# Searching step two's row tiles among eight logits per 128-column chunk, and the rest in three listed tiles

## The chip, the cores and the metric

The kernel runs on one core of a Trainium2 chip. The metric is the device time of one execution in microseconds; the number given for a kernel is the median over its runs. A profile is one further execution, recorded instruction by instruction. The engines are PE (TensorE), DVE (VectorE), ACT (ScalarE), POOL (GpSimd) and SP (SyncE, which here issues most DMAs).

## What is computed

Two graph layers over N = 4096 nodes with 256 features. Layer 0 is a dense graph attention and is not touched by the change. Layer 1 does two diffusion steps along two paths:

```python
def _top_p_attention(X, W1, W2, W3):
    q = X @ W1.T @ W2.T
    k = X @ W3.T
    logits = q @ k.T / TAU
    probs = jax.nn.softmax(logits, axis=-1)
    idx = jnp.argsort(-probs, axis=-1)
    sp = jnp.take_along_axis(probs, idx, axis=-1)
    cs = jnp.cumsum(sp, axis=-1)
    keep_sorted = cs - sp < TOP_P            # 0.9
    mask = ...                               # scattered back
    A = probs * mask
    return A / jnp.maximum(A.sum(-1, keepdims=True), 1e-12)

R = S + eye; R = R / R.sum(-1)               # S is the adjacency
for n in range(2):
    A = _top_p_attention(Xa, W1, W2, W3)
    Xf = R @ Xf                              # "mixing"
    Xa = A @ Xa                              # "row tiles"
    Z = Z + Xf @ U1[n].T + Xa @ U2[n].T
h = X + Z; layer norm; add X; layer norm
```

For each row of the attention matrix the smallest set of probabilities that sums to 0.9 (the nucleus) has to be found. On the reference's inputs a row of step one keeps 4.8 entries on average, one of step two 30 (median 12, the largest 846).

## The kernel before

`graph_attention` is layer 0. `nucleus_layer` is layer 1, and its work is laid out by a plan: `at(time, part, ...)` enters each part of each tile with a due time in units of a step-one tile, `carry_out()` sorts the entries, and the instructions of PE, ACT, DVE and POOL are issued in that order (`tc.manual_schedule`). So the due times of the dictionaries `T1`, `T2` and `TE` are an order and no clock: each engine runs its own instructions in the order written and waits on semaphores. SP has its own queue of DMAs, in the order in which the parts issue them.

Step one handles 28 row tiles as `EasyTile` (the eight largest logits of a row, gathered), then nine "dense" tiles as `RowTile(0, ...)`: the last four and five with rows that eight entries did not cover. The rows of these five are found by `HardRows`: a flag for each row, ranks by matmuls with triangular and full matrices (`count`), a list of row numbers (`place`, `enter`, `keep`, `read_list`), and an indirect DMA that gathers the listed rows (`load_hard`). A dense tile of step one computes 4096 logits a row (L1105) and keeps the eight largest of each chunk of 128 columns (`tops`, L1115). It searches the threshold among these 256 candidates alone: two estimates (`under`, L1201), a mask (`final`), three rounds of eight maxima (`sort`, L1311 and L1313), `edge`, and then one pass over all 4096 columns that keeps what reaches the edge (`select`, L1362).

Step two runs 32 tiles `RowTile(1, i)`, 128 rows each, over all 4096 columns (`place_second`). For each tile: logits, eight blocks of 512 (PE L1105, ACT L1110); the maximum over 4096 (`top`, L1122); exponentials and their sums (ACT, L1129 and L1140); three estimates of the threshold, on a quarter of the columns, on ACT's half (`estimate_half`, L1213 and L1216, four passes over 2048) and on half (`estimate`, L1201); `final`, a mask of 4096 columns into the single buffer `w`; `tops` over `w`; six rounds of `sort`; `edge`; `inside` (ranks among the 256 candidates, for ties); `cut`, which takes the kept candidates out of `w` chunk by chunk (32 replaces of eight values, L1371) and subtracts `w` from `p` on POOL (L1375, four of 1024 columns); then 32 transposes (L1383) with copies on ACT (L1396) and 32 products against `xa` (L1405, two passes each) into `ap`. `product_out` scales the rows and stores them into `xa2_d`.

Beside the tiles runs the mixing: `Group(n, g)` covers 512 columns of the adjacency; each of its 32 steps loads a block of `adj32_d` (256 KB) and one of `adj_d` in 8 bits (64 KB) into one of three buffers each (L1678), and PE does two pairs of matmuls (L1713): the rows in 16 bits against the 8-bit block, the rest against the 32-bit block. Step two holds the last six groups of the first mixing and all eight of the second. When a group of the second is done, `Out` finishes its four tiles: `product_y` and `sum_y` (the mixed part, into `h_d`), then `product` for both attention parts, two layer norms (mostly small POOL operations) and the store. At the end a count of rows whose search did not hold is read (`flag`); only if it isn't zero does a general path run after it (`missed`).

Of the kernel before, what the change touches and what calls it, by code (L numbers as in the profile page):

```python
# [8 lines left out]
F32 = mybir.dt.float32  # L9
# [13 lines left out]
P = 128  # L23
# [62 lines left out]
def tile_graph_layers(  # L86
# [60 lines left out]
    xa1_d = dram.tile([N + P, D], F32, name="xa1_d")  # L147
    src_d = dram.tile([2, H, N], F32, name="src_d")
# [8 lines left out]
    def lengthen(part):  # L157
# [13 lines left out]
        xf, room, x1_d, xa2_d, xa1_d, narrow, shares, flag, out,  # L171
# [3 lines left out]
    missed = nc.values_load(flag[0:1, 0:1], min_val=0, max_val=2 * STEPS * N)  # L175
# [642 lines left out]
ROOM = HARD * P  # L818
# [3 lines left out]
def nucleus_layer(  # L822
    ctx, tc, adjT, adj_d, adj32_d, y_d, h_d, high_d, low_d, w1, w2, w3, kT, U1T, U2T, ln_g, ln_b, ident, eps,
    xf, room, x1_d, xa2_d, xa1_d, narrow, shares, flag, out,
# [79 lines left out]
    junk_v = one.tile([P, N // 2], U8, name="junk_v")  # L904

# [3 lines left out]
    SEARCHED = FIRST + NT  # L909
# [8 lines left out]
    def spare(length):  # L918
# [21 lines left out]
    nc.gpsimd.memset(every, 1.0)  # L940
    nc.gpsimd.affine_select(
        before, every, pattern=[[1, P]], compare_op=ALU.is_gt, fill=0.0, base=0, channel_multiplier=-1
    )
    sums_before = [one.tile([P, FEW + 1], F32, name=f"sums_before{k}") for k in range(3)]
    for t in sums_before:
        nc.gpsimd.memset(t[:, 0:1], 0.0)
    is_hard = one.tile([P, EASY], F32, name="is_hard")
    nc.gpsimd.memset(is_hard, 0.0)
    BATCH = 7

    def counted(name, pattern, base, step=0):
# [6 lines left out]
    ids = counted("ids", [[P, EASY]], 1, 1)  # L958
    places = spare(P)
    nc.gpsimd.iota(  # L960
        places, pattern=[[1, P]], base=-ROOM, channel_multiplier=0, allow_small_or_imprecise_dtypes=True
    )
    steps = counted("steps", [[P, HARD - 1]], P - ROOM)
    blocks = counted("blocks", [[1, HARD]], 0)
    beyond = counted("beyond", [[0, 1]], N + 1, 1)
    listed = one.tile([P, HARD], F32, name="listed")
    hard_ids = one.tile([P, HARD], I32, name="hard_ids")
    sources = one.tile([P, HARD], I32, name="sources")
    unused = one.tile([P, HARD], F32, name="unused")
    fits = one.tile([P, 1], F32, name="fits")  # L970
# [68 lines left out]
    class RowTile:  # L1039


        def __init__(self, n, i, hard=None):
            self.n, self.i, self.hard = n, i, hard
            self.id = f"{n}_{i}" if hard is None else f"{n}_h{hard}"
            self.at = FIRST + i if n else i - EASY if hard is None else OWN + hard
            self.est = EST[n]
# [5 lines left out]
        @property  # L1052
        def own(self):
            return self.cur[:, self.i, :] if self.hard is None else hx[:, self.hard, :]
# [64 lines left out]
        def top(self):  # L1119
            self.ntop = self.tiny("ntop")  # L1120
            src = self.p if self.n else self.cand
# [30 lines left out]
        def scalars(self):  # L1152
# [10 lines left out]
            self.aim = self.tiny("aim", aims[self.n].shape[1])  # L1163
            nc.vector.tensor_scalar(self.aim, aims[self.n], self.rz, None, ALU.mult)
            self.set_goal(0)

        def scalars2(self):
            q, z = self.q_row, all_z[:, self.at, :]
            self.gain = self.tiny("gain", len(self.est) + 1)
            nc.vector.tensor_scalar(self.gain, gains[self.n], q, None, ALU.mult)  # L1170
# [4 lines left out]
            if self.n == 0:  # L1175
# [19 lines left out]
        def under(self, dst, sub=1):  # L1195

            src = self.cand if self.n == 0 else self.p
# [24 lines left out]
        def estimate(self, k):  # L1222
            self.b = self.under(junk_v, (4, None, 2)[k] if self.n else 1)
# [7 lines left out]
        def join(self, k):  # L1231
            b, share = self.b, 0 if self.n and k == 0 else None
            if self.n and k:
# [13 lines left out]
        def move(self, k):  # L1247
# [4 lines left out]
            if last and self.n:  # L1252
# [35 lines left out]
        def lift(self):  # L1288

            f = self.tiny("f")  # L1290
            nc.vector.tensor_scalar(f, self.t, self.rz, ALONE[self.n], ALU.mult, ALU.is_ge)
# [3 lines left out]

        def final(self):
            b = self.under(w)
            self.r = self.tiny("r")
            nc.vector.tensor_scalar(self.r, b, self.left, None, ALU.add)


        def sort(self, k):
            rounds = ROUNDS[self.n]
            if k == 0:
                self.src = w[:, : NC * TOP] if self.n == 0 else self.cand
                self.rest_of = two.tile(
                    [P, NC * TOP], F32, tag="left", name=f"left{self.id}", bufs=1
# [1255 lines left out]
```

## Time and profile before

| | us |
|---|---|
| median of 8 runs | 3193.47 |
| lowest, highest | 3180.82, 3209.27 |
| the profiled execution | 3194.15 |
| its span, first to last instruction | 3192.4 |

Busy time of the engines by stage of the profiled execution, in us:

| stage | window | PE | DVE | ACT | POOL | DMA share |
|---|---|---|---|---|---|---|
| graph attention | 0 to 950 | 839 | 812 | 748 | 102 | 0.67 |
| step one, easy tiles | 950 to 1325 | 333 | 328 | 282 | 246 | 0.43 |
| step one, dense tiles | 1325 to 1500 | 162 | 148 | 150 | 27 | 0.10 |
| keys of step two | 1500 to 1641 | 121 | 33 | 38 | 14 | 0.45 |
| step two | 1641 to 3192 | 1350 | 1335 | 1117 | 596 | 0.40 |

Times count from the first instruction. A row of the groups of instructions reads: line, engine, operation, what it writes and reads, shape and count, then busy us and the mean ns of one, then the engine's idle time before it and what ended that. A row of the timeline reads: start, length, engine, line, operation, names, shape and count, and in brackets idle time before it. Matmuls are pipelined, so that their rows overlap.

### The profile page before, as it was taken

Reading aid. Unit: us, or ns where it says so; the run is one execution under the profiler, and the core shown is the slowest. Engines: PE = TensorE matmul, PEld = TensorE weight load, DVE = VectorE, ACT = ScalarE, POOL = GpSimd, SP = SyncE. Lnnn points to the kernel's source line nnn. Section 1 sums busy time; section 2 is a strip of 40 time slices with the busy share of each in tenths; the row PEclk is TensorE's granted clock in tenths of the full one; section 3 lists DMA queues with packets and bytes.
Section 4 is the critical chain, followed back from the end, with each engine's and each line's share of the span. In section 5 each row is a group of like instructions: output and inputs, shape, how many; then the busy total and the mean of one; then the engine's idle time right before and its main releaser. Section 6 shows DMA issues by size and latency. Waiting matters only on the chain.

```text
span 3192.4 us, 48261 instructions
## 1 busy us (share of the span) xinstructions
PE 2804.6 (88%) x15876; PEld 1690.0 (53%) x15876; DVE 2656.4 (83%) x6811; ACT 2335.0 (73%) x3521; POOL 985.1 (31%) x1102
## 2 busy tenths in 40 slices
PE   7999887898888998699967998997998989989975
PEld 4432222222225665487634666665666766766754
DVE  4769998999987999787128999999988888888983
ACT  4668987898876787797247777778766777777762
POOL 1101141000005777412002233324235354454553
PEclk8989999999989999799988999999999999999987
DMA  9988867653214444201544444463444444444410
GB/s 240 241 203 253 223 225 244 224 195 110 86 57 125 132 138 131 76 23 51 178 140 133 131 131 128 136 193 95 127 130 133 134 135 136 138 138 137 134 54 23
DMA packets 298853, 451.68 MB, mean 141 GB/s; under 512 B 34528, under 2 KB 174816, under 8 KB 295520
## 3 DMA queue, kind: packets, MB, share of 16 engines
q1 hardware_dynamic: 278528, 401.04, 38.0%
q0 software_dynamic: 20064, 47.47, 8.8%
q8 instruction: 127, 2.08, 0.3%
q14 instruction: 134, 1.10, 0.1%
HBM read 447.06 MB, written 127.14 MB: 180 GB/s over the span
## 4 chain that ended last, share of the span: by engine, by line
PE 29%; DVE 20%; ACT 8%; POOL 4%; issue 3%; DMA 2%; SPq 0%; DVEq 0%; POOLq 0%; ACTq 0%
PE ap L1405 9%; PE rp L1713 7%; DVE w L1371 4%; DVE c L1115 2%; PE tpa L1383 2%; PE ap_h L1405 2%; DVE ntop L1122 2%; DVE junk_v L1201 2%; DVE w L1201 2%; POOL p L1375 2%; ACT junk_s L1213 1%; PE zpo L1796 1%; PE lp L1105 1%; PE ape L1513 1%; DVE tie L1466 1%
## 5 line engine op out<-in xcount | busy, mean ns | idle before, releaser
L1405 PE MATMUL ap<-xa,at 128*128 128x257 f32 x2048 | 502.4, 389 | 38.9 <-ACT at L1396 38.6
L676 DVE COPY_PREDICATED other<-mask,e 128x2048 f32<-128x2048 uint8 x176 | 453.8, 2590 | 52.9 <-ACT other L661 45.1
L1713 PE MATMUL rp<-adj,low 128*128 128x512 f32 x896 | 474.0, 591 | 9.9 <-DMA adj<-adj_d 9.7
L1405 PEld LDWEIGHTS ap<-xa,at 128*128 128x128 f32 x2048 | 383.2, 193 | 102.6 <-ACT at L1396 49.0
L654 ACT ACTIVATE e<-src,minus_flat,factors 128x2048 f32<-128x2048 f32 x176 | 367.8, 2090 | 64.8 <-DVE other L676 34.7
L706 PE MATMUL acc<-other,v 128*32 128x512 f32 x2816 | 344.4, 607 | 77.2 <-DVE other L676 58.3
L1713 PE MATMUL rp<-short,p 128*128 128x512 fp8e4 x896 | 352.6, 394 | 22.2 <-POOL short L1695 18.3
L661 ACT ACTIVATE other<-away,minus_flat 128x2048 f32<-128x2048 f32 x176 | 350.6, 1992 | 7.1 <-PE acc L706 4.5
L1375 POOL TENSOR_TENSOR p<-p,w 128x1024 f32<-128x1024 f32 x128 | 299.8, 2366 | 128.3 <-DVE w L1371 119.8
L1371 DVE MATCH_REPLACE8 w<-c,w 128x128 f32<-128x128 f32 x1024 | 267.7, 275 | 0.0
L1396 ACT COPY at<-tpa 128x512 f32<-128x512 f32 x280 | 161.4, 579 | 129.9 <-PE tpa L1383 128.8
L706 PEld LDWEIGHTS acc<-other,v 128*32 128x32 f32 x2816 | 80.6, 110 | 295.6 <-DVE other L676 137.4
L1105 PE MATMUL lp<-kT,q 128*128 128x512 f32 x576 | 185.9, 442 | 44.2 <-ACT p L1110 29.6
L1713 PEld LDWEIGHTS rp<-adj,low 128*128 128x128 f32 x896 | 180.1, 201 | 61.0 <-issue 20.1
L679 DVE COPY_PREDICATED e<-mask,away 128x2048 f32<-128x2048 uint8 x80 | 208.5, 2606 | 2.6 <-DMA mask<-mask_d 2.5
L1115 DVE MAX8 c<-w 128x8 f32<-128x128 f32 x1024 | 200.8, 275 | 0.0
L1383 PE MATMUL tpa<-ident,p 128*128 128x128 f32 x1152 | 179.0, 280 | 24.3 <-POOL p L1375 12.3
L706 PE MATMUL acc<-other,ones 128*32 128x512 f32 x1408 | 186.1, 601 | 0.0
L1129 ACT ACTIVATE junk_s<-p,htop 128x2048 uint8<-128x2048 f32 x72 | 144.3, 2004 | 48.3 <-DVE htop L1124 48.3
L1383 PEld LDWEIGHTS tpa<-ident,p 128*128 128x128 f32 x1152 | 145.5, 145 | 62.3 <-POOL p L1375 15.2
L1503 POOL DMA_INDIRECT p<-x_d,tie x152 | 158.0, 1039 | 66.2 <-issue 21.2
L1713 PEld LDWEIGHTS <-p 128*128 128x128 f16 x896 | 87.4, 98 | 166.9 <-issue 159.3
(429 smaller groups left out, 5982.2 us busy)
## 6 DMA issues: line engine op xcount, KB each, us to landing
adj<-adj_d SPq DMA_DIRECT2D x448, 256.0 KB
mask<-adj_d SPq DMA_DIRECT2D x164, 256.0 KB
short<-adj_d SPq DMA_DIRECT2D x448, 64.0 KB
adj<-in_adjT SPq DMA_DIRECT2D x64, 256.0 KB
mask<-mask_d SPq DMA_DIRECT2D x60, 256.0 KB
mask<-in_adjT POOLq DMA_DIRECT2D x32, 256.0 KB, 9.4
src<-src_d SPq DMA_DIRECT2D x8, 1024.0 KB
away<-src_d SPq DMA_DIRECT2D x8, 1024.0 KB
```

The costliest lines, as they stand in the source:

```text
L654: nc.scalar.activation(self.e, self.head.src, AF.Relu, scale=self.factor(0), bias=self.factor(2))
L661: nc.scalar.activation(self.other, self.head.away, AF.Identity, bias=self.factor(2))
L676: nc.vector.copy_predicated(self.other, self.mask, self.e)
L679: nc.vector.copy_predicated(self.e, self.mask, self.other)
L706: nc.tensor.matmul(head.acc[k][at : at + 32, :], weights, self.e[:, b * 512 : (b + 1) * 512], tile_position=(0, at), **ends,)
L1105: nc.tensor.matmul(lp, self.q[:, k], kT[:, b * 512 : (b + 1) * 512], start=k == 0, stop=k == 1)
L1115: nc.vector.max(self.cand[:, c * TOP : (c + 1) * TOP], src[:, c * CHUNK : (c + 1) * CHUNK])
L1371: nc.vector.match_replace(w[:, cols], self.cand[:, c * TOP : (c + 1) * TOP], w[:, cols], 0.0)
L1375: nc.gpsimd.tensor_tensor(self.p[:, cols], self.p[:, cols], w[:, cols], ALU.subtract)
L1383: nc.tensor.transpose(tp[:, q * P : (q + 1) * P], self.p[:, (b * 4 + q) * P : (b * 4 + q + 1) * P], ident,)
L1405: nc.tensor.matmul(self.ap[:, : D + 1], at[:, q * P : (q + 1) * P], self.cur[:, j, :], start=j == 0, stop=j == NT - 1,)
L1713: nc.tensor.matmul(self.rp[c], part, a[:, jj, :], start=j == 0 and k == 0, stop=j == NT - 1 and k == len(parts) - 1,)
```

## The change

Step two's tiles become `FewTile`: they search among the eight largest of each chunk, like the dense tiles of step one. Rows of which a chunk may hold eight or more entries of the nucleus, or whose search does not end within its three rounds, get a flag. Two lists of flagged rows are made (tiles 0 to 21, two tiles of places; tiles 22 to 31, one), and these rows are gathered, searched again as `RowTile(1, None, k)` with the search that all tiles of step two had, and their outputs are written over those of the fast tiles by indirect DMA. All rows are therefore stored in `xa1_d` in step one too, and the output is split: `Half` takes the first attention part along with the mixed part. The due times change: the mixing's pace beside the fast tiles is halved (`mix=4.5` at a `unit` of 1.385, from 2.189 at 1.9), and `mix_late` holds for groups after them.

The core of the diff:

```diff
+LATE = 3
+CUT = 22
...
+    late_d = dram.tile([LATE * P, D], F32, name="late_d")
...
+    junk_few = junk_v[:, 12 * P : 12 * P + NC * TOP]
...
+    lists = [
+        Listed(0, 0, EASY, BATCH, HARD),
+        Listed(1, 0, CUT, CUT, LATE - 1),
+        Listed(2, CUT, NT - CUT, NT - CUT, 1),
+    ]
...
+    class FewTile(RowTile):
+        def __init__(self, i):
+            super().__init__(1, 0, 0)
+            self.i, self.hard, self.few, self.id, self.at = i, None, True, f"1_{i}", FIRST + i
+            self.est = EST[0]
...
+        def flag(self):
+            high, e = all_h[:, self.at : self.at + 1], self.e
+            c = self.cand
+            nc.vector.tensor_reduce(
+                high,
+                c.rearrange("p (c k) -> p c k", k=TOP)[:, :, TOP - 1 : TOP],
+                AX.XY,
+                ALU.max,
+            )
+            part = self.tiny("flag", 6)
+            tied, more, c1, c2, above, edge = (part[:, k : k + 1] for k in range(6))
+            nc.vector.tensor_scalar(
+                junk_few, c, e, None, ALU.is_equal, ALU.add, accum_out=tied
+            )
+            nc.vector.tensor_scalar(more, tied, self.fit, None, ALU.is_gt)
+            nc.vector.tensor_scalar(edge, more, 2.0**-24, 1.0 - 2.0**-24, ALU.mult, ALU.add)
+            nc.vector.tensor_scalar(edge, edge, e, None, ALU.mult)
+            self.limit = edge
+            self.ties = self.tiny("ties", FEW)
+            nc.vector.tensor_scalar(self.ties, ranks, self.fit, e, ALU.is_lt, ALU.mult)
+            nc.gpsimd.tensor_scalar(c1, self.fit, FEW + 0.5, more, ALU.is_gt, ALU.mult)
+            nc.gpsimd.tensor_scalar(c2, self.out_of, 0.5, c1, ALU.is_lt, ALU.add)
+            nc.gpsimd.tensor_scalar(above, e, 2.0, c2, ALU.is_gt, ALU.add)
+            nc.gpsimd.tensor_scalar(c1, high, e, above, ALU.is_ge, ALU.add)
+            nc.gpsimd.tensor_scalar(
+                late_flags[:, self.i : self.i + 1], c1, 0.5, None, ALU.is_gt
+            )
+
+        def mark(self):
+            nc.vector.match_replace(w, self.ties, self.p, 2.0)
+
+        def select(self):
+            nc.vector.scalar_tensor_tensor(
+                self.p, w, self.limit, self.p, ALU.is_gt, ALU.mult
+            )
...
-    def load_hard(b):
+    def load_hard(n, b):
+        if n:
+            k = b + LATE - 1 if n == 2 else b
+            late_rows[k] = two.tile([P, D + 1], F32, tag="rows", name=f"late{k}", bufs=2)[:, :D]
         nc.gpsimd.indirect_dma_start(
-            hx[:, b, :], None, x1_d, bass.IndirectOffsetOnAxis(ap=sources[:, b : b + 1], axis=0)
+            late_rows[k] if n else hx[:, b, :],
+            None,
+            xa1_d[:N] if n else x1_d,
+            bass.IndirectOffsetOnAxis(ap=lists[n].sources[:, b : b + 1], axis=0),
         )
...
+    class LateOut(Out):
...
+        def load(self, q):
+            for to, source in ((self.x1, x1_d), (self.sums, h_d)):
+                nc.gpsimd.indirect_dma_start(
+                    to[:, q],
+                    None,
+                    source,
+                    bass.IndirectOffsetOnAxis(ap=late_sources[q], axis=0),
+                )
...
+        def send(self):
+            for q in range(LATE):
+                nc.gpsimd.indirect_dma_start(
+                    out,
+                    bass.IndirectOffsetOnAxis(ap=late_sources[q], axis=0),
+                    self.sums[:, q],
+                    None,
+                )
...
-        for i in range(NT):
-            place_second(RowTile(1, i), i)
-        length = T2["mix"]
...
+        steps = [FewTile(i) for i in range(NT)]
+        late = [RowTile(1, None, k) for k in range(LATE)]
+        steps += late
+        time, waits, unit_of = 0.0, [], {}
+        for t in steps:
+            t.waits = list(waits)
+            waits = [("w", t.id)]
+            if isinstance(t, FewTile):
+                place_few(t, time)
+                for n in (1, 2):
+                    if t.i == lists[n].first + lists[n].tiles - 1:
+                        place_list(n, time + TF["flag"] + TF["list"])
+                        if n == 2:
+                            last = time
+                        waits.append((HardRows, f"{n}_0", "enter", ()))
+                if t.i == CUT + 2:
+                    at(time, late_tables, 2, does=("tables", 2), needs=[("placed", 1)])
+                time += 1
+            else:
+                n = 2 if t.hard == LATE - 1 else 1
+                t.guard = [("placed", 2)]
+                if n == 2:
+                    time = max(time, last + TF["hard"])
+                elif not t.hard:
+                    time = max(time, last + TF["next"])
+                place_load(n, 0 if n == 2 else t.hard, time - TF["load"])
+                here = base
+                base, unit = base + unit * time, T2["unit_hard"]
+                place_second(t, 0.0)
+                base, unit = here, T2["unit"]
+                time += T2["apart_hard"]
+        fast_end = last + 1
         time = T2["mixes"]
+
+        def place_next(m):
+            nonlocal time
+            length = T2["mix" if time < fast_end + T2["turn"] else "mix_late"]
...
+        (slice(FIRST, FIRST + NT), late_flags),
```

`place_few` enters the parts of a `FewTile` in the order of step one's dense tiles (`place_first`) with `flag` and `mark` between `edge` and `select`. `Listed` holds what one list needs (its matrices, places and row numbers), `place_list` enters `HardRows` for the lists 1 and 2, and `late_out` is the one `LateOut`, entered by `place_late` after all outputs. The last line shown excuses flagged rows from the count at the end.

## The prediction

> **What bounds the kernel now.** I read the page's busy shares first, then the busy time by stage, then single instructions in order of time.
>
> ```profile
> PE 2804.6 (88%) x15876; PEld 1690.0 (53%) x15876; DVE 2656.4 (83%) x6811; ACT 2335.0 (73%) x3521; POOL 985.1 (31%) x1102
> PE   7999887898888998699967998997998989989975
> DVE  4769998999987999787128999999988888888983
> 1325.00:1500.00 175.00, 162.09 (x807) 131.25 (x806) 148.20 (x548) 150.18 (x305) 26.69 (x32) 0.95 0.10 33
> 1760.00:2300.00 540.00, 480.75 (x2285) 339.72 (x2283) 509.40 (x1990) 416.84 (x788) 167.79 (x149) 0.97 0.43 133
> 2300.00:3000.00 700.00, 643.62 (x3056) 471.90 (x3055) 610.12 (x2346) 514.35 (x1030) 315.28 (x413) 0.97 0.44 137
> ```
>
> The stage rows give window, length, then busy us of PE, PEld, DVE, ACT and POOL, the granted clock, the DMA share and GB/s. Step two, the part that is changed, runs from 1641 us (its first logits are issued at 1643.29) to the end: 1551 of 3192.4 us. PE looks busiest, but its matmuls overlap, so I count the distance from one start to the next:
>
> ```profile
> 2001.85 0.39 PE L1713 MATMUL rp<-short,p 128*128 128x512 fp8e4 x1
> 2001.88 0.58 PE L1713 MATMUL rp<-adj,low 128*128 128x512 f32 x1
> 2002.31 0.39 PE L1713 MATMUL rp<-short,p 128*128 128x512 fp8e4 x1
> ...
> 2021.94 1.91 PE L1405 MATMUL ap<-xa,at 128*128 128x257 f32 x8
> 2023.68 0.38 PE L1713 MATMUL rp<-short,p 128*128 128x512 fp8e4 x1
> ```
>
> A mixing pair costs 0.46 us (2001.85 to 2002.31), though its rows say 0.39 and 0.58. Eight product matmuls cost 1.74 us. In the same way four transposes (L1383, 2020.15 to 2020.59) cost 0.44 and four logits (L1105, 1643.29 to 1644.23) 0.94. A row tile is 64 product matmuls, 32 transposes, 16 logits and its query: 13.9 + 3.5 + 3.8 + 0.8 = 22.0 us of PE. A mixing group is 64 pairs: 29.6 us. Over all of step two, in the order in which the instructions are issued, this makes 1243 us, 80% of 1551. Between 1760 and 2300 PE has 84% by this count and DVE is busy 509.4 of 540 us, 94%: VectorE sets the pace, 42.2 us a tile (the maximum L1122 runs at 1769.0 and, 12 tiles on, at 2275.2). From 2300 on outputs stand between the tiles; DVE has 87%, PE 88%, and a tile takes 49.4 us.
>
> **What a tile loses and gains on DVE.**
>
> ```profile
> L1371 DVE MATCH_REPLACE8 w<-c,w 128x128 f32<-128x128 f32 x1024 | 267.7, 275 | 0.0
> L1115 DVE MAX8 c<-w 128x8 f32<-128x128 f32 x1024 | 200.8, 275 | 0.0
> L1375 POOL TENSOR_TENSOR p<-p,w 128x1024 f32<-128x1024 f32 x128 | 299.8, 2366 | 128.3 <-DVE w L1371 119.8
> ```
>
> The cut (32 replaces with their loads, 2012.11 to 2020.46) goes: 8.4 us. The maximum over 4096 (4.41) becomes one over 256 (0.42): 4.0. The two estimates (1.28 and 2.34) become two of 0.48: 2.7. The final mask (4.48) becomes 0.48: 4.0. Six rounds of the sort (5.3) become three (2.3): 3.0. The rank work of `inside` and the last move's extra scalars shrink by about 2.8. Together 24.9 us less. New are `mark`, a replace over 4096 columns that the trace lacks (L1371 takes 275 ns for 128, L1313 408 ns for 256, so 1.04 ns a column: estimate 4.4; bounds 2.2, were it half that per column, and 8.9, were it double), and `select`, which step one has at 4.47. Net: -16. From 509.4 / 540 x 42.2 = 39.8 us, a tile comes to 24. ACT loses four passes of 2.0 us (L1213, L1216) from 417 / 540 x 42.2 = 32.6, so about 24 remain. POOL loses 4 x 2.37 us and gets five operations of one column, 0.2 to 0.3 us each as in L1337 and L1338. PE keeps 22.0 a tile. So the bound passes from DVE to PE.
>
> The nearest precedent is step one, whose dense tiles use the same eight per chunk:
>
> ```profile
> 1408.33 4.47 DVE L1362 SCALAR_TENSOR_TENSOR p<-p,all_e 128x4096 f32<-128x4096 f32 x1
> ...
> 1431.70 4.48 DVE L1362 SCALAR_TENSOR_TENSOR p_h<-p_h,all_e 128x4096 f32<-128x4096 f32 x1
> ```
>
> One tile follows the other after 23.4 us; the six selects from 1362.8 to 1477.8 are 23.0 apart. PE's 22.1 us fill 96% of that, beside DVE at 148 / 175 = 85% and ACT at 86%. That is the share I take for the new tiles.
>
> **The sum, from 1641 us.** Ahead of it almost nothing changes (four tiles store one more 128 KB block, small reorderings): 0, with 10 us either way.
>
> 1. *The 32 tiles.* The changed order puts seven load steps of mixing (14 pairs, 6.5 us) into most tiles, half of what stands there now: 22.0 + 6.5 = 28.5 us of PE a tile. From tile 0's logits to the late tiles' first ones all PE work sums to 882 us, 851 of it before tile 31's logits. At 96.5% that is 882 us for the 851, or 29.5 a tile. DVE then has 24 / 29.5 = 81%, less than step one's 85%. The first two tiles carry only 8 and 11 us of PE; they run at DVE's pace, some 25 each, so (25 - 8) + (25 - 11) = 31, of which about 20 remains, as the first products stand behind them. Subtotal 902: tile 31 starts at 2543.
> 2. *The rest.* From there PE has 470 us: tile 31's interval (32), three full late searches (66 of PE), some 226 of the 448 mixing steps, all 32 outputs (3.9 each) and the list (some 7). Here the loads count. Each step (two pairs, 0.93 us of PE) loads 256 + 64 KB into one of three buffers, and where mixing stands alone the trace has this:
>
> ```profile
> 1661.34 0.38 PE L1713 MATMUL rp<-short,p 128*128 128x512 fp8e4 x1
> 1662.47 0.50 PE L1713 MATMUL rp<-adj,low 128*128 128x512 f32 x1 [0.76 <-DMA adj<-adj_d]
> ```
>
> SP issues 14 of these load pairs from 1649.26 to 1671.73, 1.6 us each, at a DMA share of 0.64 (window 1650 to 1672). In the new tail the bytes are 226 x 320 KB + 32 outputs x 7 x 128 KB = 104 MB. The window 2300 to 3000 moved 137 GB/s at 0.44, so full share is 311 GB/s and these bytes need 336 us; at 0.64 they take 525. PE at 0.88, as from 2300 to 3000, gives 470 / 0.88 = 534. I take 530. Bounds: 487 (PE at 96.5%, loads hidden) and 623 (every step at 1.6 us with the other 261 us of PE beside none of it).
> 3. *The end.* Four outputs and the scatter follow the last mixing: an output now takes 9 us from sum to store (3163.89 to 3172.86); the last four come some 7 us apart, then the store lands and three indirect writes follow (1.04 us each by L1503, landing after 2.5). 27 us beyond what is in the 470; 15 to 45.
>
> 1641 + 902 + 530 + 27 = 3100, 92 below the span of 3192.4. The profiled run took 3194.15, 0.7 over the median of 3193.47, so I add 1.8 and lean by 3 towards the upper bounds, which reach further: 3105.
>
> The list's `place` waits in DVE's order for `w`, free after tile 31's select; its ten blocks of 128 columns cost about 1.5 us (L1371's 1.04 ns a column), and behind it stand only late tiles and outputs, while PE has mixing to run. Cover lost: 110 us, one late search. The twelve indirect transfers on POOL (1.04 us each) lie beside idle POOL.
>
> **Rule against row.** By the spans of its matmul rows PE is the busiest engine (2804.6 us), and three more tiles at 24.8 (64 x 0.389) + 9.0 (32 x 0.280) + 7.0 (16 x 0.44) would add 122 us. Against that stands the Trainium skill, "Perfetto Trace Analysis", section "Identifying the Most-Contended Engine": matmul busy time doesn't tell how near PE is to its limit. The spacing rows agree; by busy time the forecast would be 3194 + 122 = 3316.
>
> The skill also speaks against the 1.6 us: "DMA: Bandwidth & Descriptors", section "Anatomy of one DMA", gives about 2.0 us plus bytes over 436 GB/s for a DMA from GpSimd. For 320 KB that is 2.75 us, and with three buffers an estimate of (2.75 + 0.93) / 3 = 1.2 us a step; the loads would then hide and the sum would be 43 lower. The measured row decides.
>
> **Rivals.** (a) *The loads hide*, 15%: PE at 96.5% in the rest too. For: half of the late groups also hold product work. Against: the wait above. 1641 + 902 + 487 + 27 + 1.8 = 3059. (b) *The fixed order couples three engines*, 15%, the slower side: PE, DVE and ACT at 28.5, 24 and 24 us a tile wait for each other, as from 2300 to 3000 where none passes 88%. Then a tile takes 28.5 / 0.88 = 32.4, and 30 x 2.9 = 87 more give 3192; with `mark` at its upper bound DVE's 28.5 joins PE's and 33 us a tile give 3210. It decides from 32.2 us a tile on. Against: step one ran the same tile at 96%. (c) *The lists overflow*, or another check on the rows fails, 3%: then the general path after step two runs. Its price lies outside the trace; its first part alone repeats graph attention, the stage 0 to 950: over 4100. On the reference's inputs I count 248 rows out of reach of the eight, 154 and 94 against 256 and 128 places, so the change does what it says. (d) *Half of that coupling*, 5%: 3160.
>
> **Numbers.** The forecast, 3070 to 3150, has 62%. The measurement can't tell 0.3% (10 us) from nothing. Faster: 62 + 15 (a) + 5 (d) + 3 of (b) = 85%; same: 5 of (b); slower: 7 of (b) and 3 of (c) = 10%. Range 3050 to 3190: it holds the forecast, most of (a), (d) and half of (b).
>
> **What would show it.** Right: tile 31's logits near 2540, new tiles 29 to 30 us apart, DVE near 81% there and no POOL row of 128x1024 but for the three late tiles; about 550 us after it, with PE waiting for adj. Wrong: tiles over 32 us apart, or a rest over 620 us.

## The result and the profile after

The changed kernel takes 3207.65 us, the median of 23 runs (3194.91 to 3217.50), against 3193.32 for the kernel before, the median of 65 runs beside it (3179.29 to 3212.09). The ratio is 1.0046 with a 95% interval of 1.0033 to 1.0058: slower by half a per cent, and 103 us above the forecast of 3105. The profiled execution took 3198.35 us, with a span of 3196.2.

First the page's busy shares and slices, then the busy time by stage (window, length, busy us of PE, PEld, DVE, ACT and POOL, granted clock, DMA share, GB/s):

```profile
PE 2880.3 (90%) x16326; PEld 1767.1 (55%) x16326; DVE 2333.5 (73%) x5055; ACT 2104.1 (66%) x3100; POOL 744.6 (23%) x1177
...
PE   7999888899889998699969999999999999888973
...
DVE  4769999899978999786148888888788852554212
```

```profile
1760.00:2300.00 540.00, 538.32 (x2748) 418.45 (x2747) 454.88 (x1504) 396.67 (x754) 91.63 (x194) 1.00 0.30 95
...
2545.00:3112.00 567.00, 492.18 (x2194) 328.93 (x2192) 236.63 (x812) 207.65 (x471) 198.06 (x391) 0.96 0.60 183
3112.00:3196.20 84.20, 33.86 (x110) 24.30 (x108) 19.84 (x60) 20.27 (x56) 32.77 (x68) 0.62 0.20 60
```

The first row lies within the 32 tiles: PE is full (538 of 540 us), DVE has fallen from 94 to 84%. The second row is what stands behind the tiles up to the last mixing pair. There DVE and ACT are mostly idle, the transfers run at 183 GB/s, and PE, busy by its spans for 492 us, has only 453 by the distance from start to start: 80%. The third row is the end: 84 us in which PE's rows cover 34 and the granted clock is 0.62.

The tiles themselves came as forecast. One tile's products begin 29.0 us after another's in the timeline, the median over all tiles is 29.2, and `mark`, which the trace before did not have, takes 4.41 us by its group (busy us, mean ns, idle time before):

```profile
1714.73 1.25 PE L1448 MATMUL ap<-xa,at 128*128 128x257 f32 x5
...
1743.71 1.14 PE L1448 MATMUL ap<-xa,at 128*128 128x257 f32 x4
```

```profile
L1531 DVE MATCH_REPLACE8 w<-ties,p 128x4096 f32<-128x4096 f32 x29 | 127.8, 4409 | 0.0
```

Behind the tiles seven of step two's 14 mixing groups are left; they are called groups 11 to 17 here. From its first pair to its last each takes 61 to 71 us, where before a group between the tiles took 82 to 104 and two tiles with it. What PE waits for there, and what SP's in-order queue stands on (us in total, times, longest), from the answers on waits (`rp` is the mixing's result, `adj` and `short` its blocks, `ho` an output's rows, `L1801` the loads of the blocks, `L1924` and `L1970` a load and the store of an output):

```profile
PE rp L1836 <- DMA adj<-adj_d: 36.4, 44, 3.5
PE rp L1836 <- DMA short<-adj_d: 14.8, 11, 3.5
PE rp L1836 <- POOL short L1818: 14.4, 11, 2.8
```

```profile
SPq L1801 <- PE rp L1836: 168.0, 170, 5.9
SPq L1924 <- POOL ho L1963: 36.7, 14, 6.5
SPq L1970 <- ACT ho L1952: 21.7, 14, 7.7
```

PE loses 51 us to mixing blocks that have not landed and 14 to the diagonal additions on POOL; all its other named waits in that stretch sum to 8. That is 73 of the 114 us between its own work and the time; what the other 41 are, the views don't name (some of it is a slower clock, see the last section). SP, which issues those loads, stands for 168 us with the next load in hand because PE still reads the buffer (the three buffers are full), and for 58 us behind output transfers that wait for POOL and ACT.

The end, in the timeline:

```profile
3155.54 0.42 DVE L1955 TENSOR_TENSOR ho<-zpo,ho 128x256 f32<-128x256 f32 x1 [3.04 <-PE zpo L1935]
3155.83 0.95 POOL L1987 DMA_INDIRECT late_out<-h_d,sources  x1 [0.31 <-issue]
...
3163.25 0.60 ACT L1952 ACTIVATE ho<-ho,lesso,r1ao 128x256 f32<-128x256 f32 x1 [5.79 <-POOL lesso L1951]
...
3181.53 0.58 ACT L1952 ACTIVATE ho<-ho,lesso,r1bo 128x256 f32<-128x256 f32 x1
3182.14 0.34 SPq L1970 DMA_DIRECT2D out_y<-ho  x1
3184.72 1.06 POOL L2039 DMA_INDIRECT out_y<-late_out,sources  x1 [11.14 <-DMA out_y<-ho]
3188.13 0.97 POOL L2039 DMA_INDIRECT out_y<-late_out,sources  x1 [2.36 <-issue]
3191.61 0.96 POOL L2039 DMA_INDIRECT out_y<-late_out,sources  x1 [2.51 <-DMA out_y<-late_out,sources]
```

The last output is summed at 3155.54, but its norm needs POOL, which gathers for the late tiles until 3161.8 (ACT stands 5.79 us for it); its second scaling stands behind the late ones in ACT's order until 3181.53; and three writes follow, 3.4 us from one to the next.

### The profile page after: what moved, and what is told of

Read it like the earlier page. It is cut to its first block, busy times and chain, and to the rows that moved or that the text cites. A ratio compares the mean times of both kernels' runs of the same rounds, so it can differ in the third digit from the quotient of the medians.

```text
span 3196.2 us, 47009 instructions
## 1 busy us (share of the span) xinstructions
PE 2880.3 (90%) x16326; PEld 1767.1 (55%) x16326; DVE 2333.5 (73%) x5055; ACT 2104.1 (66%) x3100; POOL 744.6 (23%) x1177
## 5 line engine op out<-in xcount | busy, mean ns | idle before, releaser
L1448 PE MATMUL ap<-xa,at 128*128 128x257 f32 x2048 | 486.8, 382 | 0.8 <-ACT at L1439 0.7
L1152 DVE MAX8 c<-p 128x8 f32<-128x128 f32 x1152 | 233.4, 277 | 14.4 <-ACT p L1147 14.3
L1147 ACT COPY p<-lp 128x512 f32<-128x512 f32 x288 | 152.5, 595 | 38.9 <-PE lp L1142 38.0
L1142 PE MATMUL lp<-kT,q 128*128 128x512 f32 x576 | 163.4, 420 | 9.3 <-ACT p L1147 9.0
L707 PE MATMUL acc<-e,v 128*32 128x512 f32 x1280 | 154.6, 601 | 8.5 <-DVE e L680 8.5
L1147 ACT COPY pe<-lpe 128x512 f32<-128x512 f32 x224 | 124.4, 600 | 35.8 <-PE lpe L1553 35.4
```

The costliest lines, as they stand in the source:

```text
L707: nc.tensor.matmul(head.acc[k][at : at + 32, :], weights, self.e[:, b * 512 : (b + 1) * 512], tile_position=(0, at), **ends,)
L1142: nc.tensor.matmul(lp, self.q[:, k], kT[:, b * 512 : (b + 1) * 512], start=k == 0, stop=k == 1)
L1147: nc.scalar.copy(self.p[:, b * 512 : (b + 1) * 512], self.lps.pop(b))
L1152: nc.vector.max(self.cand[:, c * TOP : (c + 1) * TOP], src[:, c * CHUNK : (c + 1) * CHUNK])
L1448: nc.tensor.matmul(self.ap[:, : D + 1], at[:, q * P : (q + 1) * P], self.cur[:, j, :], start=j == 0, stop=j == NT - 1,)
```

## The experiments

Profiles of the changed kernel's variants begin step two anywhere between 1638 and 1670 us, after nearly the same work, so a profile is compared from the first mixing pair of step two on. The kernel before was run beside every variant (its medians lie between 3192 and 3201), so the ratio is the safer number to compare. e1, e6, e7, e8 and e14 have two runs each, e4 three, e3 and e5 four, the others six or more. The table has for each run its median and its ratio to the kernel before; then, from its profile, the length of step two, of groups 11 to 17 (the mixing behind the tiles), what PE has in these by the distances between starts, the difference, and the time from the last mixing pair to the end, all in us. e4 and e10 change next to nothing in groups 11 to 17 and have 518 us there where the changed kernel has 512: a difference of 6 us in that column is nothing.

| run | median | ratio, 95% interval | step two | groups 11-17 | PE | difference | end |
|---|---|---|---|---|---|---|---|
| changed kernel | 3207.7 | 1.0046 (1.0033-1.0058) | 1551.8 | 511.9 | 399.6 | 112 | 83.9 |
| e1 half the loads | 3159.8 | 0.9887 (0.9849-0.9924) | 1505.1 | 469.3 | 399.6 | 70 | 84.3 |
| e2 other queues | 3194.2 | 0.9997 (0.9969-1.0025) | 1539.9 | 499.6 | 399.6 | 100 | 87.5 |
| e3 mixing earlier | 3232.4 | 1.0111 (1.0089-1.0133) | 1584.7 | 751.5 | 621.0 | 131 | 138.7 |
| e4 no late outputs | 3171.7 | 0.9927 (0.9906-0.9948) | 1529.3 | 518.1 | 399.1 | 119 | 58.2 |
| e5 diagonal on DVE | 3251.8 | 1.0184 (1.0140-1.0229) | 1602.6 | 520.0 | 399.6 | 120 | 85.2 |
| e6 no outputs | 3018.2 | 0.9453 (0.9428-0.9479) | 1370.8 | 394.3 | 293.8 | 101 | 23.2 |
| e7 no late search | 3116.7 | 0.9762 (0.9738-0.9786) | 1467.1 | 460.7 | 337.5 | 123 | 58.7 |
| e8 two buffers | 3350.5 | 1.0494 (1.0466-1.0522) | 1699.3 | 629.4 | 399.5 | 230 | 84.6 |
| e9 four buffers | 3192.0 | 0.9982 (0.9959-1.0006) | 1533.4 | 495.4 | 399.6 | 96 | 83.6 |
| e10 end reordered | 3198.7 | 1.0028 (1.0001-1.0054) | 1548.1 | 518.1 | 399.3 | 119 | 77.3 |
| e11 e2, e9 and e10 | 3182.1 | 0.9954 (0.9933-0.9975) | 1518.6 | 486.8 | 399.3 | 88 | 80.9 |
| e12 narrow transfers | 3203.2 | 1.0010 (0.9988-1.0031) | 1548.3 | 510.3 | 399.6 | 111 | 84.2 |
| e13 e11 and the list | 3176.6 | 0.9918 (0.9888-0.9948) | 1516.3 | 482.3 | 399.7 | 83 | 79.4 |
| e14 e6 and e9 | 2990.3 | 0.9353 (0.9294-0.9412) | 1316.4 | 345.5 | 294.3 | 51 | 22.6 |

**Half the loads (e1).**

```diff
         def load(self, jc):
+            if self.in_parts and jc % 2 and jc // 4 != self.g:
+                return
...
```

(The matmuls of the skipped block read the block ahead of it; that part of the edit is not shown.)

> Step two's mixing loads only every second block of adjacency rows (and all four blocks with the diagonal) and uses each loaded block twice, so that 14 of the 32 load pairs of each of the 14 groups are left out; its output is not the reference's; all matmuls, and all output transfers, stay. Theory (after tile 31 the mixing waits for its loads: they set the pace of the 71 us groups): groups without a late search, 61 to 68 us in the changed kernel, fall towards the 45 us that PE's spacings make of them, and the whole falls by 80 to 120 us, to 3090 to 3130. Rival (the fixed order couples PE, ACT, DVE and POOL through the outputs; loads are late only because buffers come free late): groups stay above 60 us and the whole stays above 3180.

3159.8: between the two, and in neither's range. PE's waits behind the tiles (2557 to 3067):

```profile
PE rp L1842 <- POOL short L1820: 22.0, 14, 3.7
PE zpo L1941 <- ACT t_o L1014: 9.1, 3, 3.8
PE zys L1898 <- ACT y L1853: 7.0, 5, 5.3
...
PE rp L1842 <- DMA adj<-adj_d: 1.6, 2, 1.2
```

The wait for loads is gone, and 42 of the 112 us with it. The other 70 do not hang on the mixing's loads: PE now waits for POOL's diagonal and ACT's copies instead (the lines of this run's `kernel.py` are shifted by two to six). Since a loaded block serves two steps here, three buffers also hold twice as many steps ahead: e1 takes the wait for loads away, and does not tell their rate from the room that they have.

**Other queues (e2).**

```diff
-            nc.sync.dma_start(self.xa2, xa2_d[self.rows, :])
+            nc.scalar.dma_start(self.xa2, xa2_d[self.rows, :])
...
-            nc.sync.dma_start(self.res, x1_d[self.rows, :])
+            nc.gpsimd.dma_start(self.res, x1_d[self.rows, :])
...
-            nc.sync.dma_start(out[self.rows, :], self.h)
+            nc.scalar.dma_start(out[self.rows, :], self.h)
```

> All loads and stores stay, but three of the seven transfers of each output leave SP's in-order queue: the store is issued by ACT behind the scaling that it waits for, the residual's load by POOL behind the addition that it waits for, the load of xa2 by ACT. Theory (mixing loads stand in SP's queue behind output transfers that wait for POOL, ACT and PE: 48.4 + 42.2 + 12.9 = 104 us of such waits after 2560): the whole falls by 30 to 90 us, to 3120 to 3180. Rival 1 (the bytes set the pace, DMA share 0.6 to 0.66 being all that is to be had): within 10 us of the changed kernel's 3208. Rival 2 (coupling of the engines): within 10 us too, or up to 20 slower from POOL's and ACT's added issues.

A gain of 12 us in the profile, 13 in the medians: below the theory's 30, next to the rivals' bound. What SP stood behind the outputs, it now mostly stands for a free buffer (216.6 us in place of 154.4 over the same stretch). The queue was a small part.

**Mixing earlier (e3).**

Three due times change, out of the long lines of `T2` (`mix`, `parts`) and `TO` (`late`):

```diff
-... mix=4.5, ... parts=0.718, ... late=36.042, ...
+... mix=2.9, ... parts=0.85, ... late=39.5, ...
```

> Only the pace of step two's mixing under the few tiles changes: one group per 2.9 tiles in place of 4.5 (11 load steps a tile in place of 7); the late outputs' place follows. Same work in all. Theory (the new tiles leave room on DMA and, with PE full there, every microsecond of mixing moved forward costs its PE time once, 30.7 us a group at 96.5%, but saves the 71 us that it takes at the end): tiles go from 29.3 to about 33.5 us apart, four groups leave the tail, and the whole falls by 60 to 120 us, to 3090 to 3150. Rival (the time is PE's total, and what is moved only moves): within 15 us of 3208.

Slower by 25, a miss for both. By stage:

```profile
1723.00:2334.00 611.00, 603.06 (x3013) 451.83 (x3012) 458.61 (x1519) 406.10 (x773) 95.36 (x216) 0.99 0.45 132
2345.00:2854.00 509.00, 467.64 (x2229) 353.30 (x2227) 324.55 (x1018) 275.41 (x564) 136.37 (x308) 0.95 0.39 114
...
3096.00:3235.00 139.00, 71.48 (x302) 57.15 (x301) 65.20 (x284) 38.57 (x94) 58.77 (x81) 0.70 0.14 42
```

The first half went as the theory had it: 33 us a tile, PE full. But with the mixing done earlier the outputs come between the tiles, where PE's share falls to 92% by spans, and the last late search stands behind the last mixing, with only outputs beside it: the end is 139 us in place of 84 (in the table groups 11 to 17 hold tiles too). This run moves three things at once, so it does not show that another pace can't win.

**No late outputs (e4).**

```diff
-        place_late(late_out, max(free + 0.1, TO["late"]), free)
```

> The outputs of the three late tiles (their gathers, products, norms and the three scattered writes) are left out, so the listed rows keep what the first search gave them. Theory (the end of the kernel is one chain: six gathers on POOL hold up the last output's norm, ACT's order puts that output's last scaling behind the late ones, and three writes follow one after the other, 3.4 us each): the whole falls by 25 to 32 us. Rival (the last four outputs' own chain ends it all anyway): by less than 10.

The end falls from 83.9 to 58.2 us, 25.7, as the theory had it. The whole is less clear: the medians differ by 36, more than the theory's 32, and step two in the profiles by 22.5. The rival falls either way. The 58 that remain are four halves and five outputs: the outputs' sums (L1955) stand about 9.3 us apart (3118.5, 3128.1, 3137.2, 3145.9, 3155.5 in the changed kernel).

**Diagonal on DVE (e5).**

```diff
-                        nc.gpsimd.tensor_tensor(part, part, diagonal, ALU.add, **kind)
+                        nc.vector.tensor_tensor(part, part, diagonal, ALU.add, **kind)
```

> The identity is added to the four diagonal blocks of each mixing group by VectorE in place of POOL, nothing else. Theory (in the tail these additions stand on POOL behind the outputs' norms, and PE waits 14.4 us for them after 2560, up to 2.8 us at once, with the clock at half afterwards): the whole falls by 10 to 25 us against the changed kernel, to 3183 to 3198. Rival (the loads are late at the same steps, and take the place of this wait): within 8 us of 3208.

Slower by 44, outside both. DVE's largest wait among the tiles (1700 to 2545):

```profile
DVE adj L1818 <- DMA adj<-adj_d: 37.4, 14, 7.6
```

There the addition waits in DVE's order for its block to land, up to 7.6 us, and once a group a tile comes 34 to 42 us after the one ahead, where it was 29 to 31. Behind the tiles nothing was gained either (difference 120): there the rival holds.

**No outputs (e6).** The plan's `place_half` and `place_out` are entered for row tile 31 alone, `place_late` not at all, and the final flag is held at 0.

> Halves and outputs of row tiles 0 to 30 and the outputs of the late tiles are left out (products, norms, loads and stores); searches, mixing and its loads stay. Theory (the mixing's loads alone set a floor, 1.6 us a step or 51 us a group, above PE's 31): groups 11 to 17 still take 48 us or more each where no late product runs in them, and the last mixing ends after 2960; in the tail SP's mixing loads wait for PE or for nothing, and PE for adj. Rival (the outputs' chains in the fixed order are what stretches the groups; without them the loads keep up with PE): groups of 31 to 40 us and the last mixing before 2900.

The mixing's last pair is at 2998, and groups 13 to 17 take 48 to 54 us, as the theory had it:

```profile
2950.00:2998.00 48.00, 35.86 (x128) 15.29 (x128) 0.00 (x0) 0.21 (x1) 3.29 (x8) 1.00 0.66 206
```

```profile
SPq L1801 <- PE rp L1836: 268.1, 229, 6.0
```

Group 17 is mixing and nothing else here: 47.8 us for 32 steps, 1.49 us a step, with 29.1 us of PE, while SP waits for buffers. And the difference is 101, nearly what it was with the outputs (112): the outputs' 106 us of PE cost 118 in the time. They lay beside none of the load waits.

**No late search (e7).**

```diff
-        steps += late
```

`place_late` is left out too, the late tiles' columns of the final count are cleared, and the final flag is held at 0.

> The three late tiles (searches, products, outputs) are left out; the lists are still counted and read. Leaving out their outputs alone made 36 us. Theory (in the tail the loads set the pace, and the late searches lie half hidden beside them): a further 25 to 45 us, to 3125 to 3147. Rival (PE sets the pace at the tail's share of 0.80): a further 66 / 0.80 = 82 us, to about 3090.

55 us below e4 by the medians, 62 by the profiles; in groups 11 to 17 it is 57 us, for 62 of PE. That is between the two and in neither's range: the searches, too, cost nearly their whole PE time.

**Two buffers (e8).**

```diff
-                self.short[jc] = rows_of(adj_d, FP8, "short", 3)
-                self.adj[jc] = rows_of(adj32_d, F32R, "adj", 3)
+                self.short[jc] = rows_of(adj_d, FP8, "short", 2)
+                self.adj[jc] = rows_of(adj32_d, F32R, "adj", 2)
```

> Mixing blocks get two buffers in place of three, in all 18 groups, nothing else. Theory (what sets the pace of the tail is the time from a freed buffer to the landed load, shared by the buffers, and not the bytes): where mixing stands alone a step takes 3 x 1.6 / 2 = 2.4 us, and the tail's groups go from 61 to 71 us to 75 to 100 us; step two grows by 50 to 170 us; tiles 2 to 31 stay at 29.3 us, since there a step comes only every 4 us. Rival (the bytes set the pace): the tail's groups stay within 3 us of what they were.

As the theory had it: 80 to 88 us a group, 147 us more in step two, and PE's waits from 2560 on are

```profile
PE rp L1836 <- DMA adj<-adj_d: 62.0, 85, 1.9
PE rp L1836 <- POOL short L1818: 36.2, 21, 4.7
PE rp L1836 <- DMA short<-adj_d: 32.3, 34, 4.3
```

Loads of 156 GB/s (2650 to 2950) in place of 187: the transfers could do more, and wait for buffers. The tiles did not quite stay: three times one comes 35 to 37 us after another.

**Four buffers (e9).** As e8 with 4, and the space for it:

```diff
-            self.q = two.tile([P, 2, P], F32R, tag="q", name=f"q_{self.id}")
+            self.q = two.tile([P, 2, P], F32R, tag="q", name=f"q_{self.id}", bufs=1)
...
-                self.cand = two.tile([P, NC * TOP], F32, tag="cand", name=f"c{self.id}", bufs=3)
+                self.cand = two.tile([P, NC * TOP], F32, tag="cand", name=f"c{self.id}", bufs=2)
...
-            cs = two.tile([P, R], F32, tag="cs", name=f"cs{self.id}")
+            cs = two.tile([P, NC * TOP], F32, tag="left", name=f"cs{self.id}", bufs=1)[:, :R]
```

> Mixing blocks get four buffers in place of three (the 2.5 KB a partition come from step two's candidates, two buffers in place of three, from its query, one in place of two, and from a scratch row that shares another's place). Theory (the time from a freed buffer to the landed load, some 4.8 us, is shared by the buffers: 2.5 us a step with two, 1.6 with three): 1.2 us with four, so that the tail's groups go from 61 to 71 us to 53 to 62 us, and the whole falls by 50 to 80 us, to 3128 to 3158, below the kernel before. Rival 1 (bytes: the transfers have all the rate there is): within 10 us of 3208. Rival 2 (the shared small buffers cost the 32 tiles more than the tail gains): tiles more than 31 us apart, 3200 or above.

18 us in the profile, 16 in the medians: a miss in size. The tiles are unharmed (29.2 us). PE's wait for loads halves from 51 to 25 us up to the last mixing (2570 to 3118):

```profile
PE rp L1836 <- DMA adj<-adj_d: 17.8, 29, 1.9
PE rp L1836 <- POOL short L1818: 14.3, 10, 3.7
PE rp L1836 <- DMA short<-adj_d: 7.5, 8, 2.5
PE zpo L1935 <- ACT t_o L1014: 5.2, 2, 3.1
```

Of these 26 us the groups get 16. The wait for the diagonal stays at 14, the other named waits grow by some 7 (the last line, PE's wait for the copy of an output's transposed block, was 2.6), and the clock is at half for 57 us of groups 11 to 17 in place of 41.

**End reordered (e10).** `LateOut.load` is split: the gathers of `x1_d` go 1.5 of a tile's time ahead, those of `h_d` ahead of the last output's sum; `finish` and `send` come behind that output's store.

> All work stays; the late tiles' outputs are placed differently: the gathers of x1 one group earlier, those of h_d ahead of the last output, and the last output's second norm ahead of the late ones. Theory (six gathers in POOL's order hold up the last output by 5.4 us, and ACT's order puts its last scaling 10 us behind): the end, 84 us from the last mixing, falls by 6 to 14 us, the whole to 3194 to 3202. Rival (the chain gathers, sums, two norms, three writes, 3.4 us each, sets the end from the last half on, wherever it stands): within 4 us of 3208.

The end is 77.3 in place of 83.9 in the profile: 6.6 us, at the low side of the theory, against the 25.7 that e4 got by leaving these outputs out. The chain itself, not its place, makes most of it.

**Together (e11).**

> Four buffers, the other queues for three of the output's transfers, and the reordered late outputs, together. Theory: the gains add in part (e2 made 13 us; with loads less late the queue matters less): 3105 to 3145, the fastest of all that keep the whole computation. Rival (they take from the same wait): no better than four buffers alone.

3182.1, 0.9954 of the kernel before: a miss, 37 us above the theory's upper end. It is 10 us below four buffers alone, but the two intervals overlap.

**Narrow transfers (e12).** Five of the seven transfers of an output have `[:, :32]` (or 16 of each 128 columns) and fixed tiles that are filled with 1.0 once.

> Five of the seven transfers of each output (y1, h, xa2, the residual, the store) move one eighth of their columns, 16 KB in place of 128; the other columns keep a constant, so the output is not the reference's. Engines' work, order and the number of transfers stay. A tail group then moves 11.6 MB in place of 13.8. Theory A (bytes: a tail group takes what its bytes take at some 200 GB/s, which is why outputs add 13 us to a group although PE waits half of the time): groups fall by a sixth, 61 to 71 us to 52 to 60 us, and the whole by 60 to 90 us, to 3118 to 3148. Theory B (PE's fixed order: while PE does an output's or a search's work, at most three steps are loaded ahead, so that work adds its own PE time to the loads' 1.6 us a step): groups within 4 us of what they were, the whole above 3180.

The bytes fell and the time did not (the first line is the changed kernel, the second this run, same window):

```profile
2650.00:2950.00 300.00, 255.76 (x1130) 170.32 (x1129) 137.84 (x490) 123.77 (x278) 111.41 (x205) 0.97 0.61 187
```

```profile
2650.00:2950.00 300.00, 257.12 (x1153) 172.76 (x1153) 137.96 (x489) 124.45 (x278) 114.29 (x210) 0.97 0.54 156
```

Theory A falls, B holds: every group is within 2 us of what it was, and the difference is 111 us as before. (By the ratios the whole is 0.4% lower, by the medians 4 us; nothing in the groups shows it.)

**The list as well (e13).** `rows.keep` and `read_list` of list 1 come 0.2 of a tile's time later.

> As e11 (four buffers, other queues, reordered end), and DVE adds list 1's rows 0.2 of a tile's time later, so that it does not stand waiting for the list's 44 matmuls (DVE idle for 12 us before L1754 in the changed kernel, tiles 20 and 21 47 us apart in place of 29). Theory: tiles 20 and 21 come to 32 to 40 us apart, 7 to 15 us less than e11, 3165 to 3177. Rival (PE itself does the 44 small matmuls for 9.4 us, at half clock, and the tile waits for that anyway): within 4 us of e11.

3176.6, 0.9918 of the kernel before (0.9888 to 0.9948), the lowest median of those that do the whole work. By the medians it is 5.5 us below e11, a little more than the rival's 4, but the intervals overlap, step two is 2 us shorter, and tiles 20 and 21 are 47.1 us apart as ever: the theory falls. By the rows the tile waits for the list itself: in the changed kernel the list's 44 small matmuls hold PE for 9.4 us, and DVE's `place` stands ahead of the next tile's maxima for 3.1:

```profile
2300.25 3.09 DVE L1728 TENSOR_TENSOR w<-junk_v,at 128x2816 f32<-128x2816 f32 x1
...
2308.57 9.39 PE L1743 MATMUL hl<-cells,w 128*128 128x2 f32 x44
```

PE stands idle for 3.9 us ahead of this, and from 2303.2 to 2323.7 its granted clock is at half.

**Four buffers without outputs (e14).**

> e9 and e6 together: four buffers for the mixing blocks, and the outputs (as in e6) left out. It asks why four buffers gave back only 18 us. Theory A (with four the loads keep up, 1.2 us a step or 38 us a group; what is left in e9 is the fixed order around the outputs): groups 13 to 17 take 38 to 46 us in place of 48 to 54, the whole 30 to 60 us less than e6's 3018. Theory B (the transfers have little more rate to give than three buffers ask of them, so that a fourth buffer mostly makes each one wait longer): groups of 46 to 52 us, the whole less than 20 us below e6.

Group 17 falls from 47.8 to 39.7 us, 1.24 a step; groups 13 to 16 to 46 to 50, of which PE has 36 to 47; 49 us less in all seven groups than e6. The transfers move 217 GB/s (2670 to 2960) where the changed kernel had 187. The medians, 28 apart, are of two runs each, whose step two began 20 us apart in the profiles. By its numbers the run lies between the theories: the medians fall by 28, just short of A's 30, and of groups 13 to 17 three are in B's range and two in A's. B's reason falls, since the transfers had more rate to give. So the fourth buffer is worth 49 us where mixing and searches stand alone, and 16 where the outputs stand among them (511.9 to 495.4); or, the other way round, the outputs' 106 us of PE cost 118 us with three buffers and 150 with four. What holds PE up around the outputs then, in place of the loads, was not separated.

## Why the prediction was wrong

The sum was 1641 + 902 + 530 + 27 = 3100 against a span of 3196.2. The profile of the changed kernel splits these 96 us by the prediction's own steps:

| step | predicted | measured |
|---|---|---|
| start to tile 31's logits | 1641 + 902 = 2543 | 2546.9 |
| PE's own work from there to the end | 470 | 474 (452 + 22.5) |
| beyond it, up to the last mixing pair | 530 - 470 = 60 | 565.4 - 452 = 114 |
| beyond it, in the end | 27 | 83.9 - 22.5 = 61 |

- **The 32 tiles** were right, the working too: 29.2 us a tile where 29.5 was said, `mark` 4.41 where 4.4 was estimated, DVE 499 of 590 us (1700 to 2290), 85% where 81 was said. One thing in them was overlooked: list 1 stands among the tiles, not behind them, and costs 18 us (47.1 between two tiles). That the sum came out within 4 us is partly luck: step two's first logits came 4 us earlier than 1641, and without the list the tiles would have taken 892 us, 10 less than said.
- **"The rest", the step that failed.** The prediction took "PE at 0.88, as from 2300 to 3000", and so let 60 us of waits stand beside 470 of work. Measured is 0.80 up to the last mixing, and 649 us from tile 31's logits to the end where about 550 was said. The share was borrowed from a stage in which a mixing step came every 3 us, so that its loads had time. Behind the tiles PE has 1.8 us of work a step on average (399.6 us for 224 steps), but 0.9 of it is mixing, which comes in runs, and then the loads set the pace: 1.49 us a step with three buffers where mixing stands alone (e6), 1.24 with four (e14); with two, and outputs between, 2.5 (e8). The prediction had this wait, from the right row, and then averaged it away: it let the late searches and outputs lie beside the loads. e6 and e7 show that they don't: in groups 11 to 17 outputs with 106 us of PE cost 118, and searches with 62 cost 57. The reading that fits is that while PE does such work at most three steps are loaded ahead, and the fourth waits as long as ever. Seven groups at 47.8 us and PE's other 196 us, one behind the other, make 530 us; measured are 512, while 0.88 would have made 454. e12 excludes the outputs' bytes as the reason. The prediction's own upper bound, "every step at 1.6 us with the other 261 us of PE beside none of it", 623 us, was the better value: by the same count 474 + 114 = 588 were measured, 58 above the 530 and 35 below the bound.
- The 470 itself was right, though the parts that the prediction names for it (32 + 66 + 226 x 0.93 + 32 x 3.9 + 7) make 440: the products of the last fast tiles, which PE does behind tile 31's logits (192 product matmuls of fast tiles there, 64 make one tile), are not among them.
- Of the 112 us in groups 11 to 17, 42 go when the loads are halved (e1); what is left lies in PE's fixed order among the outputs, with the diagonal on POOL and copies on ACT (e1, e9), and the half clock after such waits. This part is argued from the waits: how much each makes alone was not separated, since where one was taken away others took part of its place (e1, e9).
- **The end** was said as "four outputs and the scatter", 27 us beyond PE's work, and has 61. The late outputs' own chain (six gathers, two norms, three writes of 3.4 us) makes 25.7 of it (e4) and was left out but for the writes; the gathers were said to lie beside an idle POOL, and the last output's norm waits for POOL behind them. The last outputs' sums come 9.3 us apart where 7 was said.
- **Rivals.** (a), the loads hide, fell with the first group. (b) gave 3192 to 3210, and the time lies there, but not for its reason: the tiles are not coupled (PE 538 of 540 us). The coupling sat behind them. (c): nothing runs after step two. (d) fell with (b).
- **Rule against row.** The two totals decide nothing here: by matmul busy time 3316 was forecast, 108 us too much, by spacings 3105, 103 too little. The late searches decide: 122 us by busy time, 66 by spacings, and 57 measured (e7). So matmul busy time did not tell how near PE was to its limit, which is what the Trainium skill's "Perfetto Trace Analysis", section "Identifying the Most-Contended Engine", says of it. The estimate of 1.2 us a step with three buffers, worked out from the Trainium skill's "DMA: Bandwidth & Descriptors", section "Anatomy of one DMA", did not come: e6 has 1.49, near the row's 1.6, and 1.24 took four buffers (e14).

So the change did what it says: it took 13 us from a tile (42.2 to 29.2, with half the mixing beside it). The gain went into mixing that had been hidden beside VectorE's search and now stands alone, with outputs in between, and into a longer end.

## What to carry to other kernels

Work that is hidden beside a slow stage has to be priced anew when that stage gets fast: not by its share of an engine, but by what it takes when it stands alone (here 1.5 us a step for 0.9 of PE). Where a stream of loads has a few buffers, other work of the waiting engine can add to it rather than fill its gaps (here 106 us of it cost 118, and 62 cost 57); how many buffers would end that no run here shows. And a borrowed busy share holds only for the mix of work that it was read from; where a bound and an average disagree, ask which of them has the same mix.

## What had not been expected

- The granted clock falls to half in pieces of 3.4 us after waits of PE: 11 times (once for 6.8), 41 us in all, between 2545 and 3112 in the changed kernel; 154 us in groups 11 to 17 with two buffers, none in e14. In the 3.4 us ahead of each of the 11 PE's rows leave 1.6 to 3.0 us idle, and a mixing pair takes 0.88 us in such a piece in place of 0.46. So a wait can cost more than its length. But this is not what the change added: in the kernel before, the seven last mixing groups (2304 to 3045) have 44 us of it.
- The diagonal addition takes 0.28 to 0.29 us on DVE and 0.41 to 0.46 on POOL, and yet DVE was the wrong place: the wait for the block that comes with it is what counts.
- With three buffers and 14 of 32 load pairs left out (e1), SP still waits 106 us for free buffers: what keeps them full is the order of PE's work, not the queue.
